# Relu work of a graph-attention layer spread over three engines instead of two

## The chip, the cores and the metric

The kernel runs on one core of a Trainium2 chip. The metric is the device time of one execution in microseconds. The core has a matrix engine (TensorE, in the profile PE for matmuls and PEld for weight loads), VectorE (DVE), ScalarE (ACT), GpSimd (POOL) and a queue that issues transfers (SP). Each engine takes its own instructions in order; semaphores hold an instruction until what it reads is there and the buffer that it writes is free.

## The reference

64 graphs (batches) of 256 nodes with 128 features pass four layers. All share one 256 x 256 matrix `adj`. Before each layer the features are normalised and clamped, and each layer's result is added to its input. All values are float32.

```python
for layer in (L0, L1, L2, L3):
    h = maximum(layernorm(x), 0)
    x = x + layer(h)

# in each layer below, x and the first h are the normalised input
# L0, five steps; both message matrices are adj, so the halves of w3, w4, w5 can be summed
m  = adj @ h
z  = sigmoid(m @ w3.T + b3 + h @ u3.T + bu3)
r  = sigmoid(m @ w4.T + b4 + h @ u3.T + bu3)
hv = tanh(m @ w5.T + b5 + (r * h) @ u5.T + bu5)
h  = (1 - z) * h + z * hv

# L1
c1 = adj.T @ x;  c2 = 2 * adj.T @ c1 - x
out = relu([x, c1, c2, c1, c2] @ Theta1 + bias)

# L2
y = (adj @ x + x) @ weight + bias;  out = y / max(norm(y), 1e-12)

# L3, e over 256 channels; W is adj: W1, W2 are its left and right 128 columns
s1 = x @ W1.T;  s2 = x @ W2.T
pre[i, j, e] = s1[i, e] + s2[j, e] + b_lin[e]
score[i, j]  = sum_e a[e] * leaky_relu(pre[i, j, e], 0.2) + adj[i, j]
out = sigmoid(softmax(score, axis=j) @ x)
```

The bulk of the work is in `score`: for every batch 256 x 256 pairs (i, j), each with 256 channels e.

## The kernel before

Two batches form a pair, 512 tokens, and 32 pairs follow one another. A token-major tile is [token % 128, batch, token // 128, feature], a feature-major one [feature, batch, token]; a [128, 512] float32 product fills one PSUM bank.

`front(p)` is a generator that computes layers 0 to 2 of a pair and, for layer 3, `s1` and `s2` (feature-major, one tile for each half k of e). In a gate step of layer 0 (lines 246 to 275) PE makes `pm`, ScalarE copies it to `mT`, PE makes `pr` and `pz` from `mT` and `hT`, ScalarE takes two sigmoids (`r`, `z`), VectorE makes `rh`, PE makes `pv`, ScalarE takes the tanh (`hv`), VectorE makes the new `hT` with a subtraction, a product and an addition (lines 265 to 268), and PE transposes it back (`pt`).

`scores(p, background)` does the bulk. leaky(v) is written as 0.2 v + 0.8 relu(v). The linear part is separable and opens the PSUM tile `pe` with six matmuls (lines 398 to 404). For the second part a slot, one r and one half k of e, handles four rows i (g = 0 to 3, 32 rows apart) of both batches: eight instructions of 256 columns write a [128, 4, 2, 256] tile `rl`, with `s1[i]` as a scalar of each partition. Every third slot is ScalarE's (line 415), the other two VectorE's (line 417). PE then reduces over e with four matmuls (line 421), one for each 32-column group of the array; a window of weights that is zero but for one column puts row i into its place. Six `rl` buffers are shared by both engines. With 32 pairs, two halves of i, 32 values of r and two halves of e there are 4096 slots. What the text calls a row is one r: two slots.

After each row `background()` advances two generators by one stage: `tail` (softmax, weighted sum and output of a finished half of i) and `front` of the next pair. So the front of pair p + 1 is interleaved with the scores of pair p; a gate step has five stages and spans five rows. The tile framework then orders the instructions of every engine with a model of its own of when operands are ready, so a background step need not stand exactly at its row.

The activation functions in use are Sqrt (norms, row norms of layer 2), Sigmoid, Tanh and Exp. Relu and copies are in line between them. Where the function set changes, a table load stands ahead of the activation. `norm_relu` (lines 166 to 182) computes statistics, Sqrt on ScalarE, a reciprocal, four scalings and a clamp on VectorE.

Of the kernel before, what the change touches and what calls it, by code (L numbers as in the profile page):

```python
# [8 lines left out]
F32 = mybir.dt.float32  # L9
AF = mybir.ActivationFunctionType  # L10
OP = mybir.AluOpType
# [4 lines left out]
NB = 2  # batches handled together: 512 tokens, one PSUM bank per [128, 512] product  # L16
# [3 lines left out]
ALPHA = 0.2  # L20


@with_exitstack
def kernel(
# [22 lines left out]
    """Four pre-norm residual graph layers over x [B, 256, 128].  # L47

    Every batch is independent, so a pair of batches goes through all four
    layers on chip. Token-major tiles are [token % 128, batch, token // 128,  # L50
    feature]; feature-major ones are [feature, batch, token].

    The last layer's scores sum a_e * leaky(s1[i, e] + s2[j, e]) over e. With
    leaky(p) = ALPHA * p + (1 - ALPHA) * relu(p) the first part is separable,
    and the second is relu on the vector and scalar engines (e on partitions,
    j along the free axis, s1[i] as the per-partition scalar), reduced over e
    by the tensor engine: a stationary [128, 32] window, zero but for one
    column that holds (1 - ALPHA) * a, puts row i into its place in PSUM.
    """
# [9 lines left out]
    relu_pool = ctx.enter_context(tc.tile_pool(name="relu", bufs=6))  # L69
    ps = ctx.enter_context(tc.tile_pool(name="ps", bufs=6, space=PSUM))  # L70
# [16 lines left out]
    ident = const.tile([P, P], F32, name="ident")  # L87
    make_identity(nc, ident)
    eps_t = const.tile([P, 1], F32, name="eps_t")
    nc.vector.memset(eps_t, LN_EPS)  # L90

    adj_n = const.tile([P, NC, N], F32, name="adj_n")  # [n, c, m]: adj[c * 128 + n, m]
    nc.sync.dma_start(adj_n, adj.rearrange("(c p) m -> p c m", p=P))
    adj_t = const.tile([P, NC, N], F32, name="adj_t")  # [m, c, n]: adj[n, c * 128 + m]
    adj_ti = const.tile([P, NC, N], F32, name="adj_ti")  # the same of adj + I
# [8 lines left out]
    def load_transposed(w, name):  # L104
        """w [128, D] or [128, 2 * D] -> its transpose, the halves summed (both multiply the same message)."""
# [11 lines left out]
        nc.vector.tensor_copy(t, pt)  # L117
# [4 lines left out]
    w4t = load_transposed(w4_w, "w4t")  # L122
    w5t = load_transposed(w5_w, "w5t")
    u5t = load_transposed(u5_w, "u5t")
# [7 lines left out]
    nc.vector.tensor_add(gate_b[:, 2:3], braw[:, 2:3], braw[:, 4:5])  # L132
    bz, br, bh = gate_b[:, 0:1], gate_b[:, 1:2], gate_b[:, 2:3]
# [25 lines left out]
    a_lin = const.tile([P, NE, N], F32, name="a_lin")  # L159
    nc.vector.memset(a_lin, ALPHA)  # L160
    for k in range(NE):
        nc.vector.tensor_scalar(win[:, k, 31:32], acol[:, k:k + 1], 1.0 - ALPHA, None, op0=OP.mult)
        nc.vector.tensor_scalar(a_lin[:, k, :], a_lin[:, k, :], acol[:, k:k + 1], None, op0=OP.mult)

# [1 line left out]
    def norm_relu(src, h):  # L166
        """h = relu(layernorm(src)) over the features, token-major."""
# [7 lines left out]
        std = work.tile([P, NB * NC], F32, name="std")  # L175
        nc.scalar.activation(std, mv[:, :, 1], AF.Sqrt, bias=eps_t, scale=1.0)
        rstd = work.tile([P, NB * NC], F32, name="rstd")
        nc.vector.reciprocal(rstd, std)
# [3 lines left out]
        nc.vector.tensor_scalar(hh, hh, 0.0, None, op0=OP.max)  # L182

    def to_feature(h, name):
        """Token-major -> feature-major, in PSUM."""
        pt = bank([P, NB, NC, P], name)
        for b in range(NB):
            for c in range(NC):
                nc.tensor.transpose(pt[:, b, c, :], h[:, b, c, :], ident)  # L189
        return pt.rearrange("p b c n -> p b (c n)")  # L190

    def to_token(ht, name):
        """Feature-major -> token-major, in PSUM."""
# [6 lines left out]
    def mix_nodes(h, a, name):  # L200
        """[f, b, n] = sum over nodes m of h[b, m, f] * a[m, n], in PSUM."""
# [6 lines left out]
    def project(pairs, name):  # L208
        """[o, b, n] = sum of w[f, o] * t[f, b, n] over the pairs (w, t), in PSUM."""
# [6 lines left out]
    def project_token(pairs, name):  # L216
        """[n, b, c, o] = sum of t[f, b, n] * w[f, o] over the pairs (t, w), in PSUM."""
# [16 lines left out]
    def front(p):  # L234
        """Layers 0 to 2 of pair p and the operands of layer 3; yields between its stages."""
        x0 = XIN.pop(p)

        # layer 0: gated message passing
# [7 lines left out]
        for step in range(STEPS):  # L246
# [4 lines left out]
            pr = project([(w4t, mT), (u3t, hT)], "pr")  # L251
            pz = project([(w3t, mT), (u3t, hT)], "pz")
            r = feat("r")
            nc.scalar.activation(r, pr, AF.Sigmoid, bias=br, scale=1.0)  # L254
            z = feat("z")
            nc.scalar.activation(z, pz, AF.Sigmoid, bias=bz, scale=1.0)  # L256
            rh = feat("rh")
            nc.vector.tensor_mul(rh, r, hT)  # L258
            yield
# [4 lines left out]
            # (1 - z) * h + z * hv = h + z * (hv - h)  # L264
            nc.vector.tensor_sub(hv, hv, hT)  # L265
            nc.vector.tensor_mul(hv, hv, z)
            hT_new = feat("hT")
            nc.vector.tensor_add(hT_new, hT, hv)
# [11 lines left out]
        # layer 1: Chebyshev hops; both hop families use adj, so their weights are summed  # L280
# [28 lines left out]
        # layer 2: (adj + I) h W + bias, rows normalised  # L309
# [14 lines left out]
        nc.vector.tensor_mul(sq, y, y)  # L324
# [160 lines left out]
```

## Time and profile before

| what | value |
|---|---|
| device time, median of 3 runs | 7429.68 us (7429.2 to 7431.93) |
| span of the profiled execution, first to last instruction | 7427.2 us |
| median less span | 2.5 us |
| busy VectorE | 6813.8 us |
| busy ScalarE | 5601.2 us |
| busy PE, as the profile models it | 7242.1 us |
| busy GpSimd | 0.7 us |
| mean granted TensorE clock | 0.995 |
| HBM read and written | 9.70 and 8.39 MB, 2 GB/s over the span |

The profiled execution's own time is its span and what lies around it; the table sets the span beside the median of the runs. In the groups of the profile a line reads: source line, engine, operation, the tile that it writes and the tiles that it reads, shapes, count, then busy microseconds in total and mean nanoseconds of one, then the idle time just before such instructions and what ended it. Instructions on one engine overlap a little, so busy time divided by the count, the distance, is less than the mean. Each float32 matmul appears as two records. The ends of matmuls are modelled, so the busy time of PE can hold waiting. Transfers are small here (2 GB/s) and are not looked at further.

### The profile page before, as it was taken

The numbers are of one execution on the slowest core, as the hardware profiler recorded it, in microseconds if no ns is written. First come the engines' busy times: TensorE is split into PE (matmuls) and PEld (weight loads), VectorE is DVE, ScalarE is ACT, GpSimd is POOL, SyncE is SP. The second block draws the span as 40 slices with busy tenths as digits, with TensorE's granted clock in tenths as the row PEclk, the third lists the DMA queues.
The fourth block names the chain that finished last, engine by engine and source line by source line (L and its number), as shares of the span: only waits on it lengthen the run. The fifth ranks groups of instructions, "written<-read, shape, count | busy, mean of one in ns | idle before, by whom it ended". The sixth has DMA issues, their size and how long they took to land.

```text
span 7427.2 us, 120750 instructions
## 1 busy us (share of the span) xinstructions
PE 7242.1 (98%) x40713; PEld 2490.1 (34%) x40713; DVE 6813.8 (92%) x25298; ACT 5601.2 (75%) x12837; POOL 0.7 (0%) x6
## 2 busy tenths in 40 slices
PE   6999999999999999999999999999999999999999
PEld 3333333333333333333333333333333333333333
DVE  4998999999999999998999999999989999999999
ACT  3777777778777777777777777777877777777777
POOL 0000000000000000000000000000000000000000
PEclk8999999999999999999999999999999999999999
DMA  0000000000000000000000000000000000000000
GB/s 13 3 4 4 3 2 3 4 4 3 2 4 3 4 3 2 4 3 4 4 3 3 3 4 4 3 2 4 3 4 3 2 4 3 4 2 2 2 2 3
DMA packets 38816, 25.83 MB, mean 3 GB/s; under 512 B 3504, under 2 KB 38192, under 8 KB 38192
## 3 DMA queue, kind: packets, MB, share of 16 engines
q1 hardware_dynamic: 35088, 17.05, 0.8%
q8 instruction: 319, 5.23, 0.3%
q14 instruction: 305, 2.50, 0.1%
q10 hardware_dynamic: 3104, 1.05, 0.1%
HBM read 9.70 MB, written 8.39 MB: 2 GB/s over the span
## 4 chain that ended last, share of the span: by engine, by line
PE 87%; DVE 12%; ACT 1%; issue 0%; DMA 0%; SPq 0%; ACTq 0%; DVEq 0%
PE pe L421 58%; PE pm L205 7%; DVE rl L417 6%; PE pr L212 4%; PE pz L212 4%; PE pv L212 4%; PE pe L403 2%; PE pe L399 2%; PE pt L197 2%; DVE h L180 1%; PE po L222 1%; PE po L381 1%; PE pa L212 1%; PE pb L212 1%; DVE stats L173 1%; PE pt L189 1%
## 5 line engine op out<-in xcount | busy, mean ns | idle before, releaser
L417 DVE TENSOR_SCALAR rl<-s,s 128x256 f32<-128x256 f32 x21848 | 5868.7, 347 | 46.8 <-PE pe L421 44.5
L421 PE MATMUL pe<-rl,win 128*32 128x512 f32 x32768 | 5102.9, 599 | 93.4 <-DVE rl L417 93.4
L415 ACT ACTIVATE rl<-s,s 128x256 f32<-128x256 f32 x10920 | 4531.2, 497 | 399.6 <-PE pe L421 394.5
L421 PEld LDWEIGHTS pe<-rl,win 128*32 128x32 f32 x32768 | 1295.7, 109 | 3162.2 <-DVE rl L417 1569.0
L205 PE MATMUL pm<-adj_t,h 128*128 128x256 f32 x1280 | 336.0, 400 | 2.8 <-ACT h L274 2.8
L258 DVE TENSOR_TENSOR rh<-r,hT 128x512 f32<-128x512 f32 x160 | 109.8, 686 | 237.9 <-ACT r L254 237.3
L205 PEld LDWEIGHTS pm<-adj_t,h 128*128 128x128 f32 x1280 | 232.4, 195 | 166.3 <-issue 78.0
L249 ACT COPY mT<-pm 128x512 f32<-128x512 f32 x160 | 93.7, 586 | 155.3 <-PE pm L205 154.3
L254 ACT ACTIVATE r<-pr,gate_b 128x512 f32<-128x512 f32 x160 | 109.9, 687 | 114.5 <-PE pr L212 114.5
L369 ACT ACTIVATE sc<-sc,nmx 128x256 f32<-128x256 f32 x128 | 64.5, 504 | 157.3 <-DVE nmx L365 156.8
L212 PE MATMUL pr<-mT,w4t 128*128 128x512 f32 x320 | 178.9, 641 | 3.5 <-ACT mT L249 3.5
L212 PE MATMUL pv<-mT,w5t 128*128 128x512 f32 x320 | 179.5, 643 | 0.0
L403 PE MATMUL pe<-a_lin,s 128*128 128x256 f32 x512 | 168.6, 419 | 0.0
L212 PE MATMUL pr<-hT,u3t 128*128 128x512 f32 x320 | 167.3, 604 | 0.0
L212 PE MATMUL pz<-mT,w3t 128*128 128x512 f32 x320 | 165.9, 600 | 0.0
L212 PE MATMUL pv<-rh,u5t 128*128 128x512 f32 x320 | 164.5, 595 | 0.0
L262 ACT ACTIVATE hv<-pv,gate_b 128x512 f32<-128x512 f32 x160 | 108.7, 680 | 73.1 <-PE pv L212 73.0
L212 PE MATMUL pz<-hT,u3t 128*128 128x512 f32 x320 | 163.4, 592 | 0.0
L256 ACT ACTIVATE z<-pz,gate_b 128x512 f32<-128x512 f32 x160 | 109.3, 683 | 64.8 <-PE pz L212 64.8
L265 DVE TENSOR_TENSOR hv<-hv,hT 128x512 f32<-128x512 f32 x160 | 109.7, 686 | 37.7 <-ACT hv L262 36.3
L403 PEld LDWEIGHTS pe<-a_lin,s 128*128 128x128 f32 x512 | 80.9, 188 | 181.4 <-issue 179.8
L399 PE MATMUL pe<-s,a_lin 128*128 128x512 f32 x256 | 141.1, 640 | 0.0
(108 smaller groups left out, 3577.9 us busy)
## 6 DMA issues: line engine op xcount, KB each, us to landing
xin<-in_x_dram SPq DMA_DIRECT2D x64, 128.0 KB, 2.2
out_dram<-o SPq DMA_DIRECT2D x64, 128.0 KB, 1.8
w_raw<-in_L_gnn_w_w_dram ACTq DMA_DIRECT2D x3, 128.0 KB, 2.6
th_raw<-in_L_gnn_Theta_dram ACTq DMA_DIRECT2D x1, 320.0 KB, 3.4
adj_n<-in_adj_dram SPq DMA_DIRECT2D x1, 256.0 KB, 4.7
w_raw<-in_L_gnn_u_w_dram ACTq DMA_DIRECT2D x2, 64.0 KB, 2.6
bias<-in_L_gnn_bias_dram ACTq DMA_DIRECT2D x2, 64.0 KB, 3.5
w<-in_L_gnn_weight_dram ACTq DMA_DIRECT2D x1, 64.0 KB, 3.1
```

Source lines behind the costliest of these rows:

```text
L197: nc.tensor.transpose(pt[:, b, c, :], ht[:, b, c * P:(c + 1) * P], ident)
L205: nc.tensor.matmul(pm[:, b, :], h[:, b, c, :], a[:, c, :], start=(c == 0), stop=(c == NC - 1))
L212: nc.tensor.matmul(pp.rearrange("p b n -> p (b n)"), w, t.rearrange("p b n -> p (b n)"), start=(k == 0), stop=(k == len(pairs) - 1))
L254: nc.scalar.activation(r, pr, AF.Sigmoid, bias=br, scale=1.0)
L256: nc.scalar.activation(z, pz, AF.Sigmoid, bias=bz, scale=1.0)
L258: nc.vector.tensor_mul(rh, r, hT)
L265: nc.vector.tensor_sub(hv, hv, hT)
L399: nc.tensor.matmul(flat, a_lin[:, k, :P], s2[k].rearrange("p b n -> p (b n)"), start=(k == 0), stop=False, skip_group_check=True)
L403: nc.tensor.matmul(pe[:, b, :], s1[k][:, b, ic * P:(ic + 1) * P], a_lin[:, k, :], start=False, stop=False, skip_group_check=True)
L415: nc.scalar.activation(rl[:, g, b, :], s2[k][:, b, :], AF.Relu, bias=sc, scale=1.0)
L417: nc.vector.tensor_scalar(rl[:, g, b, :], s2[k][:, b, :], sc, 0.0, op0=OP.add, op1=OP.max)
L421: nc.tensor.matmul(flat[g * 32:(g + 1) * 32, :], win[:, k, 31 - r:63 - r], rl[:, g].rearrange("p b n -> p (b n)"), start=False, stop=(r == ...
```

## The change

The layer-3 slots. Half k = 0 of e is done on VectorE in one instruction of 2048 columns. With s1n = -(s1 + b), relu(s1 + b + s2) = max(s2, s1n) - s1n; the last term is linear and goes into the folded terms. Its operand `s2a` stays in PSUM, in a pool of two banks of its own; `s1n` is read with a stride of zero along j. Half k = 1 goes to ScalarE as before (eight instructions) or, in 11 of 32 rows, to GpSimd, which adds and then clamps 2048 columns, both in SBUF. `rl` now has three buffers for each of the three producers.

The linear terms. One matmul with `g2` opens `pe`; the terms that depend only on i come from four one-column matmuls with `g1` and a constant `c_b` (`crow`) and are added in `tail`.

The activation table. Sigmoid becomes 0.5 tanh(v / 2) + 0.5 with the factors folded into weights, biases and the next step; Sqrt and reciprocal become a power of -0.5 on GpSimd. Exp, Tanh, Relu, Identity and copies are left.

The gates. `pz` is not computed on its own: `pr` is kept in its bank, and one matmul with w34 = w3 - w4 is added to it after `r` was read. `hv - hT` moves from VectorE to GpSimd, as do the clamp of `norm_relu`, the square and the clamp of layer 2, and the last addition of `tail`, whose result the output transfer waits for.

PSUM banks for the front go from six to four.

```diff
+POOL_ROWS = [r for r in range(32) if r * 11 % 32 < 11]
...
-    relu_pool = ctx.enter_context(tc.tile_pool(name="relu", bufs=6))
-    ps = ctx.enter_context(tc.tile_pool(name="ps", bufs=6, space=PSUM))
+    relu_pool = ctx.enter_context(tc.tile_pool(name="relu", bufs=3))
+    ps = ctx.enter_context(tc.tile_pool(name="ps", bufs=4, space=PSUM))
+    ps_s = ctx.enter_context(tc.tile_pool(name="ps_s", bufs=2, space=PSUM))
...
+    w34 = const.tile([P, P], F32, name="w34")
+    nc.vector.tensor_sub(w34, w3t, w4t)
...
+    for k in range(NE):
+        nc.tensor.matmul(pt, adj_n[:, k, P:2 * P], a_rep[:, k, :], start=(k == 0), stop=(k == NE - 1))
+    g2 = const.tile([P, P], F32, name="g2")
+    nc.vector.tensor_scalar(g2, pt, ALPHA, None, op0=OP.mult)
...
     def norm_relu(src, h):
...
-        nc.scalar.activation(std, mv[:, :, 1], AF.Sqrt, bias=eps_t, scale=1.0)
-        nc.vector.reciprocal(rstd, std)
+        nc.gpsimd.tensor_scalar(rstd, mv[:, :, 1], LN_EPS, None, op0=OP.add)
+        nc.gpsimd.tensor_tensor(rstd, rstd, minus_half, op=OP.pow)
...
-        nc.vector.tensor_scalar(hh, hh, 0.0, None, op0=OP.max)
+        nc.gpsimd.tensor_scalar(hh, hh, 0.0, None, op0=OP.max)
...
-            pr = project([(w4t, mT), (u3t, hT)], "pr")
-            pz = project([(w3t, mT), (u3t, hT)], "pz")
+            pr = project([(u3t, hT), (w4t, mT)], "pr")
             r = feat("r")
-            nc.scalar.activation(r, pr, AF.Sigmoid, bias=br, scale=1.0)
+            nc.scalar.activation(r, pr, AF.Tanh, bias=br, scale=0.5)
+            rh = feat("rh")
+            nc.vector.scalar_tensor_tensor(rh, r, 1.0, hT, op0=OP.add, op1=OP.mult)
+            yield
+            nc.tensor.matmul(pr.rearrange("p b n -> p (b n)"), w34, mT.rearrange("p b n -> p (b n)"),
+                             start=False, stop=True, skip_group_check=True)
             z = feat("z")
-            nc.scalar.activation(z, pz, AF.Sigmoid, bias=bz, scale=1.0)
+            nc.scalar.activation(z, pr, AF.Tanh, bias=bz, scale=0.5)
...
-            nc.vector.tensor_sub(hv, hv, hT)
-            nc.vector.tensor_mul(hv, hv, z)
+            nc.gpsimd.tensor_sub(hv, hv, hT)
+            nc.vector.scalar_tensor_tensor(hv, z, 1.0, hv, op0=OP.add, op1=OP.mult)
             hT_new = feat("hT")
-            nc.vector.tensor_add(hT_new, hT, hv)
+            nc.vector.scalar_tensor_tensor(hT_new, hv, 0.5, hT, op0=OP.mult, op1=OP.add)
...
-        nc.vector.tensor_mul(sq, y, y)
+        nc.gpsimd.tensor_mul(sq, y, y)
...
-        nc.scalar.activation(nrm, nrm, AF.Sqrt)
-        nc.vector.reciprocal(rn, nrm)
+        nc.gpsimd.tensor_tensor(rn, rn, minus_half, op=OP.pow)
...
+        nc.scalar.activation(s1n, pa, AF.Identity, bias=nblin[:, 0:1], scale=-1.0)
...
+        s2a = ps_s.tile([P, NB, N], F32, name="s2a")
+        nc.tensor.matmul(s2a.rearrange("p b n -> p (b n)"), adj_t[:, 1, 0:P], hT.rearrange("p b n -> p (b n)"),
+                         start=True, stop=True)
...
-            nc.vector.tensor_add(t[:, b, :], pe[:, b, :], adj_n[:, ic, :])
+            nc.vector.scalar_tensor_tensor(t[:, b, :], pe[:, b, :], crow[:, b * NC + ic:b * NC + ic + 1], adj_n[:, ic, :],
+                                           op0=OP.add, op1=OP.add)
...
-            nc.scalar.activation(o[:, b, :], po[:, b, :], AF.Sigmoid, scale=rs[:, b:b + 1])
-        nc.vector.tensor_add(o, o, x3[:, :, ic, :])
+            nc.scalar.activation(o[:, b, :], po[:, b, :], AF.Tanh, scale=rs[:, b:b + 1])
+        nc.gpsimd.tensor_scalar(o, o, 0.5, 0.5, op0=OP.mult, op1=OP.add)
+        nc.gpsimd.tensor_add(o, o, x3[:, :, ic, :])
...
+            nc.tensor.matmul(flat, g2, hT3.rearrange("p b n -> p (b n)"),
+                             start=True, stop=False, skip_group_check=True)
+            for r in range(32):
+                i0 = ic * P + r
                 for k in range(NE):
+                    e = "v" if k == 0 else "g" if r in POOL_ROWS else "s"
+                    rl = relu_pool.tile([P, 4, NB, N], F32, name="rl_" + e)
+                    if e == "s":
+                        for g in range(4):
+                            for b in range(NB):
+                                nc.scalar.activation(rl[:, g, b, :], s2b[:, b, :], AF.Relu,
+                                                     bias=s1b[:, b, i0 + g * 32:i0 + g * 32 + 1], scale=1.0)
+                    else:
+                        whole = [P, 4, NB, N]
+                        rows = (s1b if k else s1n)[:, :, i0:i0 + 97:32].rearrange("p b g -> p g b").unsqueeze(3)
+                        in0 = (s2b if k else s2a).unsqueeze(1).to_broadcast(whole)
+                        in1 = rows.to_broadcast(whole)
+                        if e == "v":
+                            nc.vector.tensor_tensor(rl, in0, in1, op=OP.max)
+                        else:
+                            nc.gpsimd.tensor_add(rl, in0, in1)
+                            nc.gpsimd.tensor_scalar(rl, rl, 0.0, None, op0=OP.max)
```

## The prediction

> **What bounds the kernel now.** I read the busy times first, then the groups of instructions, the waits, one gate step on the timeline, and three stages of one pair by windows.
>
> ```profile
> PE 7242.1 (98%) x40713; PEld 2490.1 (34%) x40713; DVE 6813.8 (92%) x25298; ACT 5601.2 (75%) x12837; POOL 0.7 (0%) x6
> L417 DVE TENSOR_SCALAR rl<-s,s 128x256 f32<-128x256 f32 x21848 | 5868.7, 347 | 46.8 <-PE pe L421 44.5
> L421 PE MATMUL pe<-rl,win 128*32 128x512 f32 x32768 | 5102.9, 599 | 93.4 <-DVE rl L417 93.4
> L415 ACT ACTIVATE rl<-s,s 128x256 f32<-128x256 f32 x10920 | 4531.2, 497 | 399.6 <-PE pe L421 394.5
> ```
>
> The 98% of PE misleads. A slot (four rows, one half of e) is 8 matmul records, so L421 took 5102.9/4096 = 1.25 us a slot on average; the timeline below has 32 records in 3.64 us, 0.91 us a slot. The waits say why:
>
> ```profile
> PEld pe L421 <- DVE rl L417: 1569.0, 3674, 2.5
> DVE rh L258 <- ACT r L254: 237.3, 51, 10.6
> ```
>
> PE's weight loads wait for VectorE's tiles; VectorE hardly waits for buffers (44.5 us). VectorE spends 8 x 268.6 ns = 2.15 us on a slot and has two of three slots.
>
> ```profile
> 3149.16 5.07 DVE L417 TENSOR_SCALAR rl<-s,s 128x256 f32<-128x256 f32 x19
> 3152.26 1.02 PE L212 MATMUL pv<-rh,u5t 128*128 128x512 f32 x2
> 3153.21 3.64 PE L421 MATMUL pe<-rl,win 128*32 128x512 f32 x32
> 3153.33 0.68 ACT L262 ACTIVATE hv<-pv,gate_b 128x512 f32<-128x512 f32 x1
> 3154.16 0.68 DVE L265 TENSOR_TENSOR hv<-hv,hT 128x512 f32<-128x512 f32 x1
> 3156.78 0.66 PE L197 MATMUL pt<-ident,hT 128*128 128x128 f32 x4
> ```
>
> A gate step repeats every 17.19 us (mT at 3144.06, then 3161.25), five rows long, with PE and VectorE both gapless. The chain hv, hT, pt has no slack.
>
> ```profile
> 3125.04:3211.00 85.96, 85.91 (x526) 30.77 (x529) 79.04 (x276) 72.65 (x163) 0.00 (x0) 1.00 0.01 3
> 3211.00:3267.90 56.90, 53.21 (x302) 19.63 (x294) 52.62 (x205) 40.12 (x92) 0.00 (x0) 1.00 0.03 8
> 3267.90:3343.20 75.30, 75.30 (x425) 23.71 (x423) 75.30 (x291) 58.59 (x140) 0.00 (x0) 1.00 0.00 1
> ```
>
> Columns: stretch, length, busy PE, PEld, DVE, ACT, POOL. These are the gates of the next pair, its layers 1 to 3, and rows with no front left. The last stretch is VectorE alone, 100%. Scores start at 138 us, the last pair alone takes 183 us; the 31 pairs between take (7427 - 138 - 183)/31 = 229.2 us each.
>
> **The change, part by part.**
>
> *VectorE.* Out go L417 (5868.7), one subtraction of each gate step (109.7), the norms' max (53.9), reciprocals (27.5), the squares and their clamp (26.9), the output add (26.8) and the s1 copies (47.9); 652 us stay. In come 2048 maxima of 2048 columns. A row pair prices them:
>
> ```profile
> L386 DVE TENSOR_TENSOR o<-o,x 128x256 f32<-128x256 f32 x64 | 26.8, 418 | 44.9 <-ACT o L385 44.9
> L265 DVE TENSOR_TENSOR hv<-hv,hT 128x512 f32<-128x512 f32 x160 | 109.7, 686 | 37.7 <-ACT hv L262 36.3
> ```
>
> 268 ns for 256 columns more, so 686 + 6 x 268 = 2.29 us; consecutive L417 overlap by 347 - 269 = 78 ns, so 2.21 us apart. PSUM as a source costs nothing visible (L363 reads it at 422 ns). VectorE: 652 + 2048 x 2.21 + 15 = 5193 us, 1620 less. But a waiting step now stands behind a 2.2 us block where it stood behind 0.27.
>
> *ScalarE.* 21 of 32 rows of the second half: 1344 slots x 3.32 = 4462 us, 69 less. All 285 table loads (365.7 us at 1.283) but the first go, as do the square roots (45); three projections' moves instead of two and the bias forms add 25. About 5146 us. These loads sat beside VectorE's work; I give them nothing but 5 us at the start.
>
> *PE.* A gate step has five projections for six: 17.19 - 0.91 = 16.28 us. Opening a half of the scores needs one matmul for six, 240 us less in all, in stretches where VectorE set the pace: nothing.
>
> *GpSimd.* It had six instructions; now 704 slots, each a sum and a clamp of 2048 columns, and the moved small steps. Two rows bound it:
>
> ```profile
> masks.py:197 POOL MEMSET ident<- 128x128 f32 x1 | 0.2, 204 | 0.3 <-POOLq L471 0.3
> masks.py:199 POOL TENSOR_SCALAR_AFFINE_SELECT ident<-ident 128x128 f32<-128x128 f32 x1 | 0.3, 292 | 0.1
> ```
>
> With some 99 ns fixed (a memset of one column), they give 0.83 and 1.52 ns a column: a clamp of 1.8 to 3.2 us, a sum, which reads twice, 3.5 to 6.3. The select does arithmetic but ran once, cold; I take the middle, 2.5 + 4.9 = 7.4 us (5.3 to 9.5). At these middle rates the moved steps cost 14 us a pair (six two-input steps of 512 columns at 1.3, four clamps at 0.7, the outputs 2.2, small ones 1.5). GpSimd: 22 x 7.4 + 14 = 177 us a pair, or 5670.
>
> The Trainium skill, GPSIMD Engine Reference, section "Elementwise — side-by-side cycle accounting", measures 4497 ns for such a sum of 2048 float32 columns and advises VectorE for elementwise work. No run here shows it; by it the sum below would be some 180 us less, about 6650.
>
> *Buffers, queues, start.* The six shared tile buffers become three for each producer, and the front has four PSUM banks for six. VectorE waited 44.5 us for buffers in the whole run, and three maxima ahead cover three rows, 7 to 8 us: nothing, as long as no wait is longer; a longer one is priced with the waits. The 64 output transfers (1.8 us each) now follow GpSimd's add instead of VectorE's; only the last is on the path, within the 10 us I keep for the end. At the start, 138 us before, the chain loses four table loads (5 us), gains five hand-overs to GpSimd (0.6 us of longer subtraction and 0.2 each, 4 us) and the small matmuls of the folded constants behind the loads (4 us): 141.
>
> *New waits.* Each gate step goes ACT hv, then GpSimd, then VectorE. Queued behind GpSimd's wait are its next slots; behind VectorE's, the next maxima, then PE. The built order has 3.6 rows on PE between pv and pt, 3.6 x 1.82 = 6.6 us. Against that: hv 0.9, subtraction 1.4, product 0.7, one max 2.2, hT 0.7, hand-overs 0.4: 6.3. It just fits. What GpSimd's reads do to VectorE's while both run, no row shows: nothing at the low end, a whole instruction of the other engine at the high end. At the high end the product waits out a sum (4.9), hT in seven of ten steps another (4.2): 23.8 us a step. I take half a sum, 2.4 us a step, 0.8 for each of its three two-input steps, because hand-overs leave GpSimd moments between instructions.
>
> The row that bears on this: L417 moves 256 columns in 347 ns, L386 takes 418. The Trainium skill, SBUF — State Buffer, section "Who interferes with whom", says that a VectorE instruction with two SBUF inputs, or in a two-port mode, and a GpSimd instruction lock each other out for a whole instruction, while one SBUF input does not contend. The max from PSUM keeps to that; the gate products do not. By the rule the high end holds: about 7790.
>
> *Sum by stage of a pair.* Gates, 25 rows: 5 x (16.28 + 2.4) = 93.4 (86.0 before). Layers 1 to 3 now lie beside 21 rows: PE 38.6 + 16.6 = 55.2; VectorE 46.4 + 9.0 = 55.4; GpSimd 7.2 slots, 53.5, plus 4.4 of moved steps, plus three norms where it waits for VectorE's scalings behind half a max (2.2 each): 64.5; five two-input steps at 0.8: 68.5. Free, 18 rows: GpSimd 11/32 x 7.4 = 2.55 a row against 2.21 (VectorE), 2.18 (ACT), 1.82 (PE): 45.9 + 2.2 = 48.1. Together 210.0 for 229.2. Whole: 141 + 31 x 210.0 + 64 x 2.55 + 10 = 6824 span, plus the 2.5 us between span (7427.2) and median (7429.7): 6826.
>
> **Rivals.**
> 1. No port wait and a slot of 5.3 us: PE bounds the gates (81.4), VectorE the rest (58 + 39.8): 179.2 a pair, 5850; with slots of 7.4, 194.0 and 6330. For it: the chain fits in 6.6 us. Against it: four engines at 160 to 177 us a pair must never miss each other.
> 2. Slower, by one mechanism: VectorE's gate products stand behind whole GpSimd sums. 119 + 74 + 48 = 241 a pair, 7790. It decides from 229 on, that is where the wait reaches 6.2 us a step (2.4 taken). For it: hT to pt had no slack before. Against: nothing in the trace shows such blocking.
> 3. GpSimd at its upper row, 9.5 us a slot: 22 x 9.5 + 14 + 7 = 231 a pair, 7520. For it: the select is the nearest kind of instruction; against: it ran once.
> 4. The max is not what it says, PSUM or not, and excludes GpSimd: 141 + 177 = 318 a pair, over 10,000.
>
> **How the numbers follow.** Forecast (6450 to 7200) 0.44; rival 1 0.25; rival 2 0.19; rival 3 0.08, half of it slower; rival 4 0.04. Within 0.2%, which is what a measurement of this kernel tells from no change: 0.02, taken from rivals 2 and 3. Faster 0.44 + 0.25 + 0.04 = 0.73, slower 0.25. The range 6100 to 7800 leaves out rival 4, the top of rival 2 and the bottom of rival 1, about 2 in 10.
>
> **What would show it.** Maxima at 2.29 us; sums and clamps of 7.4 us together; no table loads after the first; 25 gate rows in 93 us; gate products of 0.69 us. Products of 3 to 5 us mean rival 2; GpSimd busy over 95%, rival 3; maxima far over 2.3, rival 4. The prediction is wrong if the steps stretch past 23 us or GpSimd's slot past 9.

## The result and the profile after

The changed kernel takes 9438.7 us (9438.55 to 9439.15, four executions) against 7430.7 for the kernel before in the same comparison: 1.270 times as long, interval 1.269 to 1.272. The forecast was 6826 us in a range that ended at 7800. The profiled execution has a span of 9437.0 us and its own time is 9438.78. The period of a pair went from 229.2 to 293.5 us.

Busy time of each engine (microseconds, share of the span, instructions), and the chain of work that ended last, by engine and by line:

```profile
PE 6567.8 (70%) x40021; PEld 2324.1 (25%) x40021; DVE 6394.3 (68%) x4964; ACT 5153.1 (55%) x12257; POOL 7095.6 (75%) x2182
...
POOL 49%; PE 29%; DVE 14%; issue 6%; ACT 1%; DMA 0%; POOLq 0%; ACTq 0%; DVEq 0%
```

VectorE fell from 92% to 68% and ScalarE from 75% to 55%, and no engine took their place: GpSimd, with 49% of the chain the most of any engine, is busy 75%. So the engines wait for each other. VectorE's groups, with the mean duration of one instruction (ns) after the comma:

```profile
L467 DVE TENSOR_TENSOR rl_v<-s2a,s1n 128x2048 f32<-128x2048 f32 x2048 | 4607.5, 2280 | 1088.2 <-PE pe L473 1083.0 <-PE s2a L393 5.0
L307 DVE SCALAR_TENSOR_TENSOR hT<-hv,hT 128x512 f32<-128x512 f32 x160 | 370.9, 2318 | 0.5
L293 DVE SCALAR_TENSOR_TENSOR rh<-r,hT 128x512 f32<-128x512 f32 x160 | 321.9, 2012 | 103.2 <-ACT r L291 103.2
L305 DVE SCALAR_TENSOR_TENSOR hv<-z,hv 128x512 f32<-128x512 f32 x160 | 294.5, 1841 | 96.9 <-POOL hv L304 96.9
```

And GpSimd's:

```profile
L470 POOL TENSOR_SCALAR rl_g<-rl_g 128x2048 f32<-128x2048 f32 x704 | 3850.9, 5470 | 55.8
L469 POOL TENSOR_TENSOR rl_g<-s2b,s1b 128x2048 f32<-128x2048 f32 x704 | 2551.9, 3625 | 1350.1 <-PE pe L473 1342.0 <-ACT s2b L398 4.8
```

Three things stand here. The max takes what it was priced at, 2.28 us. A slot on GpSimd takes 3.62 + 5.47 = 9.1 us, and its clamp is the longer half. And the three gate steps on VectorE, 0.69 us each before, take 1.8 to 2.3 us in the mean. Two more readings follow, first the waits (total, times, longest):

```profile
ACT rl_s L459 <- PE pe L473: 1522.2, 633, 15.2
...
POOL rl_g L469 <- PE pe L473: 1342.0, 277, 8.9
DVE h L218 <- POOL rstd L216: 1155.3, 96, 22.6
...
PEld pt L227 <- POOL h L220: 1065.2, 95, 24.3
```

VectorE waits for the norms' `rstd`, 12 us at a time in the mean and up to 22.6. PE's wait for the clamped `h` is for the most part the same stretch seen from PE. Layer 2 waits 7 us for its squares (218.1 us in 32 waits); meanwhile ScalarE and GpSimd run out of buffers, which PE frees. The first norm of a pair waits longest, here as a group and once on the timeline (start, duration):

```profile
L218 DVE TENSOR_SCALAR h<-xin,mv,rstd 128x128 f32<-128x128 f32 x128 | 35.9, 343 | 681.1 <-POOL rstd L216 681.1
```

```profile
4242.11 0.17 DVE L213 BATCH_NORM_AGGREGATE mv<-stats 128x2 f32<-128x6 f32 x1
...
4242.88 5.36 POOL L470 TENSOR_SCALAR rl_g<-rl_g 128x2048 f32<-128x2048 f32 x1
...
4266.25 0.23 POOL L215 TENSOR_SCALAR rstd<-mv 128x4 f32<-128x4 f32 x1
...
4267.63 1.12 DVE L218 TENSOR_SCALAR h<-xin,mv,rstd 128x128 f32<-128x128 f32 x4 [22.62 <-POOL rstd L216]
```

The statistics are ready at 4242.28 us. GpSimd then makes a clamp and two whole slots more before it takes `rstd`. The norm's own clamp does not queue: it starts 0.09 us after the scalings (4268.84 us). Then the timeline of one gate step:

```profile
4084.90 3.62 POOL L469 TENSOR_TENSOR rl_g<-s2b,s1b 128x2048 f32<-128x2048 f32 x1 [4.07 <-PE pe L473]
4085.01 4.06 DVE L293 SCALAR_TENSOR_TENSOR rh<-r,hT 128x512 f32<-128x512 f32 x1
...
4088.61 5.68 POOL L470 TENSOR_SCALAR rl_g<-rl_g 128x2048 f32<-128x2048 f32 x1
...
4097.30 3.62 POOL L469 TENSOR_TENSOR rl_g<-s2b,s1b 128x2048 f32<-128x2048 f32 x1 [1.76 <-PE pe L473]
...
4098.38 3.08 DVE L307 SCALAR_TENSOR_TENSOR hT<-hv,hT 128x512 f32<-128x512 f32 x1
...
4101.61 0.63 PE L235 MATMUL pt<-ident,hT 128*128 128x128 f32 x4 [2.73 <-DVE hT L307]
```

`rh` starts 0.11 us after a sum on GpSimd and ends 0.55 us after that sum; `hT` starts inside the next sum and ends 0.54 us after it. Both spent the sum waiting. The max, with one operand in PSUM, is never held up so: the longest of the 2048 takes 2.29 us. The stages of one pair by windows (the columns as before; the last three are the granted clock, the DMA share and GB/s):

```profile
3982.40:4103.00 120.60, 98.95 (x529) 33.41 (x532) 85.83 (x40) 70.24 (x160) 87.11 (x25) 0.89 0.01 2
4103.00:4209.50 106.50, 66.45 (x430) 27.03 (x423) 72.73 (x80) 53.98 (x132) 78.29 (x29) 0.82 0.02 4
4209.50:4276.00 66.50, 39.63 (x302) 11.94 (x305) 41.84 (x35) 36.84 (x93) 56.41 (x15) 0.82 0.00 1
```

| stage | before | forecast | measured |
|---|---|---|---|
| gates | 86.0 | 93.4 | 120.6 |
| layers 1 to 3 | 56.9 | 68.5 | 106.5 |
| free rows | 75.3 | 48.1 | 66.5 |
| sum | 218.2 (pair 229.2) | 210.0 | 293.6 |

The windows of before lie in a pair of 223.5 us (the pairs take 223.5, 233.1 and 230.7 us in turn) and end 5.3 us short of it; those of the changed kernel cover their pair whole. Only the free rows gained. Of the 83.6 us over the forecast, 27.2 lie in the gates, 38.0 in layers 1 to 3 and 18.4 in the free rows, which end with the 22.6 us wait for `rstd` shown above.

### The profile page after: what moved, and what is told of

Its sections match the earlier page's. It is cut to its first block, busy times and chain, and to the rows that moved or that the text cites. A ratio compares the mean times of both kernels' runs of the same rounds, so it can differ in the third digit from the quotient of the medians.

```text
span 9437.0 us, 102574 instructions
## 1 busy us (share of the span) xinstructions
PE 6567.8 (70%) x40021; PEld 2324.1 (25%) x40021; DVE 6394.3 (68%) x4964; ACT 5153.1 (55%) x12257; POOL 7095.6 (75%) x2182
## 3 DMA queue, kind: packets, MB, share of 16 engines
q10 hardware_dynamic: 3104, 1.05, 0.0%
## 4 chain that ended last, share of the span: by engine, by line
POOL 49%; PE 29%; DVE 14%; issue 6%; ACT 1%; DMA 0%; POOLq 0%; ACTq 0%; DVEq 0%
POOL rl_g L470 26%; POOL rl_g L469 17%; PE pe L473 12%; PE pm L243 7%; DVE rl_v L467 5%; DVE hT L307 4%; DVE x L372 3%; PE pr L250 3%; PE pt L235 2%; POOL h L220 2%; DVE hv L305 1%; POOL hv L304 1%; PE pv L250 1%; POOL rstd L216 1%; PE pa L250 1%
## 5 line engine op out<-in xcount | busy, mean ns | idle before, releaser
L467 DVE TENSOR_TENSOR rl_v<-s2a,s1n 128x2048 f32<-128x2048 f32 x2048 | 4607.5, 2280 | 1088.2 <-PE pe L473 1083.0
L459 ACT ACTIVATE rl_s<-s2b,s1b 128x256 f32<-128x256 f32 x10752 | 4435.1, 496 | 1532.7 <-PE pe L473 1522.2
L470 POOL TENSOR_SCALAR rl_g<-rl_g 128x2048 f32<-128x2048 f32 x704 | 3850.9, 5470 | 55.8
L469 POOL TENSOR_TENSOR rl_g<-s2b,s1b 128x2048 f32<-128x2048 f32 x704 | 2551.9, 3625 | 1350.1 <-PE pe L473 1342.0
L473 PE MATMUL pe<-rl_v,win 128*32 128x512 f32 x16384 | 2861.2, 645 | 796.9 <-DVE rl_v L467 794.1
L473 PE MATMUL pe<-rl_s,win 128*32 128x512 f32 x10752 | 1976.4, 647 | 0.0
L473 PEld LDWEIGHTS pe<-rl_v,win 128*32 128x32 f32 x16384 | 544.6, 114 | 2340.0 <-DVE rl_v L467 1353.7
L473 PE MATMUL pe<-rl_g,win 128*32 128x512 f32 x5632 | 976.9, 616 | 76.6 <-POOL rl_g L470 76.6
L473 PEld LDWEIGHTS pe<-rl_s,win 128*32 128x32 f32 x10752 | 431.7, 118 | 906.2 <-issue 833.6
L218 DVE TENSOR_SCALAR h<-xin,mv,rstd 128x128 f32<-128x128 f32 x128 | 35.9, 343 | 681.1 <-POOL rstd L216 681.1
L218 DVE TENSOR_SCALAR h<-x,mv,rstd 128x128 f32<-128x128 f32 x384 | 106.7, 341 | 474.2 <-POOL rstd L216 474.2
L307 DVE SCALAR_TENSOR_TENSOR hT<-hv,hT 128x512 f32<-128x512 f32 x160 | 370.9, 2318 | 0.5
```

The costliest lines, as they stand in the source:

```text
L307: nc.vector.scalar_tensor_tensor(hT_new, hv, 0.5, hT, op0=OP.mult, op1=OP.add)
L459: nc.scalar.activation(rl[:, g, b, :], s2b[:, b, :], AF.Relu, bias=s1b[:, b, i0 + g * 32:i0 + g * 32 + 1], scale=1.0)
L467: nc.vector.tensor_tensor(rl, in0, in1, op=OP.max)
L469: nc.gpsimd.tensor_add(rl, in0, in1)
L470: nc.gpsimd.tensor_scalar(rl, rl, 0.0, None, op0=OP.max)
L473: nc.tensor.matmul(flat[g * 32:(g + 1) * 32, :], win[:, k, 31 - r:63 - r], rl[:, g].rearrange("p b n -> p (b n)"), start=False, stop=(r == ...
```

## The experiments

Three theories came from these lines. Queue: the moved small steps stand behind 9.1 us slots in GpSimd's order. Port: VectorE's steps that read SBUF stand still while GpSimd reads it. Price: 22 slots of 9.1 us are 200 us a pair, too many by themselves. A time given without an interval below is of one execution. An edit also shifts the order in which the framework places PE's work, so a difference of some tens of us is not read as an effect.

### Queue and Port, each alone and together

**e1_steps_back**: GpSimd keeps its slots, the small steps go back.

```diff
-        nc.gpsimd.tensor_scalar(rstd, mv[:, :, 1], LN_EPS, None, op0=OP.add)
-        nc.gpsimd.tensor_tensor(rstd, rstd, minus_half, op=OP.pow)
+        std = work.tile([P, NB * NC], F32, name="std")
+        nc.scalar.activation(std, mv[:, :, 1], AF.Sqrt, bias=eps_t, scale=1.0)
+        nc.vector.reciprocal(rstd, std)
...
-        nc.gpsimd.tensor_scalar(hh, hh, 0.0, None, op0=OP.max)
+        nc.vector.tensor_scalar(hh, hh, 0.0, None, op0=OP.max)
...                          # likewise hv - hT, sq, rn and the output's two steps
```

> All small steps go back from GpSimd to where they were before (subtraction, clamps, square, output addition on VectorE, the roots as Sqrt on ScalarE with a reciprocal, so table loads return); GpSimd keeps only its 704 slots. Queue theory (the small steps stood behind 9.05 us slots in GpSimd's order: VectorE waited 1155 us for the norms' roots, 218 for the squares, 161 for the row norms, PE 983 for the clamps): some 50 to 60 us a pair of 294 go, 7600 to 8000. Port theory (VectorE's steps with two SBUF inputs stand still while GpSimd reads): blocked steps stay and become more, 8900 to 9400. Price theory (22 slots of 9.05 us, 199 us a pair, are GpSimd's floor): floor 6500, the run follows whichever of the other two is left.

Measured: 8793 us, 645 less, in neither range. VectorE's groups say why:

```profile
L219 DVE TENSOR_SCALAR h<-x,mv,rstd 128x128 f32<-128x128 f32 x384 | 790.2, 2432 | 0.1
L308 DVE SCALAR_TENSOR_TENSOR hT<-hv,hT 128x512 f32<-128x512 f32 x160 | 394.9, 2468 | 0.5
...
L425 DVE TENSOR_SCALAR sums<-sums 128x2 f32<-128x2 f32 x64 | 210.4, 3288 | 26.2 <-ACT sc L422 26.2
```

The norm's scalings took 0.34 us each in the changed kernel, since GpSimd then stood waiting for their result. Now GpSimd runs slots beside them, and they take 2.4 us. The queue's wait went; the blocked time that it had kept away came.

**e5_one_pass**: the small steps stay on GpSimd; its slot becomes eight instructions that add and clamp in one pass.

```diff
+                    if e == "g":
+                        for g in range(4):
+                            for b in range(NB):
+                                nc.gpsimd.tensor_scalar(rl[:, g, b, :], s2b[:, b, :],
+                                                        s1b[:, b, i0 + g * 32:i0 + g * 32 + 1], 0.0,
+                                                        op0=OP.add, op1=OP.max)
...
-                            nc.gpsimd.tensor_add(rl, in0, in1)
-                            nc.gpsimd.tensor_scalar(rl, rl, 0.0, None, op0=OP.max)
...
```

> GpSimd makes its slots in one pass, eight instructions of 256 columns that add a scalar of each partition and clamp, in place of a sum (3.62 us) and a clamp (5.36 us) of 2048. By the moved output step (0.405 us for 256 columns of multiply and add) a slot costs 3.3 us, by the clamps (1.50 us for 512) 6.0. Price theory: 66 to 125 us a pair less of GpSimd work, shorter pieces ahead of each small step and each VectorE step, 7500 to 8300. Port theory: VectorE's steps wait for pieces of 0.4 to 0.75 us instead of 3.6: gate steps under 1.3 us. Queue theory: waits for the roots fall with the piece length, from 7 to 8 us to under 2, if the order lets a small step between pieces; if it stands behind a whole slot, they fall to 3 to 6.

Measured: 8914 us, 525 less and short of the range. The slot is no cheaper, but VectorE is free:

```profile
L459 POOL TENSOR_SCALAR rl_g<-s2b,s1b 128x256 f32<-128x256 f32 x5632 | 6417.1, 1170 | 1120.2 <-PE pe L475 1115.3
...
L293 DVE SCALAR_TENSOR_TENSOR rh<-r,hT 128x512 f32<-128x512 f32 x160 | 124.4, 777 | 107.4 <-ACT r L291 107.4
...
L218 DVE TENSOR_SCALAR h<-x,mv,rstd 128x128 f32<-128x128 f32 x384 | 106.9, 341 | 556.6 <-POOL rstd L216 556.6
```

Eight distances of 6417.1/5632 = 1.14 us make 9.1 us a slot. VectorE's total falls from 6394 to 5468 us with the same instructions: 927 us of the changed kernel were blocked time. What remains is the queue: the scalings still wait 1220 us for `rstd`.

**e4_psum_gates**: `r`, `z` and the gated product lie in PSUM, so that each gate step of VectorE reads one tile of SBUF. Nothing is moved from GpSimd.

```diff
-            r = feat("r")
-            nc.scalar.activation(r, pr, AF.Tanh, bias=br, scale=0.5)
+            pv = bank([P, NB, N], "pv")
+            nc.scalar.activation(pv, pr, AF.Tanh, bias=br, scale=0.5)
             rh = feat("rh")
-            nc.vector.scalar_tensor_tensor(rh, r, 1.0, hT, op0=OP.add, op1=OP.mult)
+            nc.vector.scalar_tensor_tensor(rh, pv, 1.0, hT, op0=OP.add, op1=OP.mult)
...                          # likewise z and the product hv
```

> Only the gates change: r, z and the gated difference lie in PSUM banks, so each of VectorE's three gate steps has one SBUF input; GpSimd's work and order are as in the changed kernel. Port theory: rh, hv and hT fall from 2.0, 1.8 and 2.3 us to 0.7, a gate step from 24.6 to about 19 us, 25 to 28 us a pair, 8600 to 8700. Queue theory: the steps fall or not, but the time does not, since the chain waits for GpSimd anyway: 9300 to 9440.

Measured: 8924 us, 514 less, between the ranges. The mechanism shows in full beside the same long sums:

```profile
L373 DVE SCALAR_TENSOR_TENSOR x<-y,rn,x 128x128 f32<-128x128 f32 x128 | 247.5, 1991 | 160.8 <-POOL rn L369 160.8
...
L293 DVE SCALAR_TENSOR_TENSOR rh<-pv,hT 128x512 f32<-128x512 f32 x160 | 109.5, 685 | 117.6 <-ACT pv L291 117.6
L308 DVE SCALAR_TENSOR_TENSOR hT<-pv,hT 128x512 f32<-128x512 f32 x160 | 108.8, 680 | 0.2
```

The steps whose second operand moved take 0.68 us again; layer 2's addition, left with two SBUF operands, still takes 1.99. It is where the operands lie, not the operation.

**e6_steps_pass**: the edits of e1 and e5 together.

> The two experiments that each took away one delay are put together: the small steps are off GpSimd, as where it keeps only its slots (8793 us), and its slot is eight one-input instructions of 256 columns, as in that run (8914 us). If the two delays simply add, 9439 - 645 - 525 = about 8270 us. If each was the other's cover (a step freed of the queue still stood behind a whole sum or clamp), what is left is the price of a slot: 22 x 9.0 to 9.4 us = 198 to 207 us a pair, so 138 + 31 x 198 to 215 + 205 = about 6500 to 7100 us, with VectorE's products, its four scalings and the factor two on the sums under 1 us each.

Measured: 6682 us, as the second reading expected; a pair takes 204.7 us.

| | small steps on GpSimd | small steps back |
|---|---|---|
| slot of two long instructions | 9439 | 8793 |
| slot of eight short ones | 8914 | 6682 |

Each edit alone is worth 525 or 645 us, both together 2756. Each delay covered the other. What is left is the price:

```profile
PE 5959.8 (89%) x40021; PEld 2156.9 (32%) x40021; DVE 5681.8 (85%) x5604; ACT 5401.6 (81%) x12606; POOL 6450.9 (97%) x5638
```

GpSimd is busy 97%, 22 x 9.16 = 202 of 204.7 us a pair. VectorE's total is 1878 us below that of e1 (7560), which differs in the form of GpSimd's slot alone: so much was blocked time there.

### Length, operation, and which of the small steps

**e10_short_pieces**: as e6, but sum and clamp stay two passes, each cut into eight.

```diff
-                            nc.gpsimd.tensor_add(rl, in0, in1)
-                            nc.gpsimd.tensor_scalar(rl, rl, 0.0, None, op0=OP.max)
+                            for g in range(4):
+                                for b in range(NB):
+                                    nc.gpsimd.tensor_add(rl[:, g, b, :], in0[:, g, b, :], in1[:, g, b, :])
...                          # then eight clamps of rl[:, g, b, :] in two such loops
```

> The small steps are off GpSimd; its slot is the sum and the clamp of the changed kernel, each cut into eight instructions of 256 columns. It separates the length of GpSimd's instruction from its form. If a blocked VectorE step waits for the end of the GpSimd instruction that is running, no wait is longer than 0.4 to 0.8 us (a 256-column piece of a sum of 3.6 us or a clamp of 5.4 us, plus its fixed part): rh, hv, hT and the scalings stay under 1.3 us in the mean, and the time is that of a price of 9.5 to 10.5 us a slot, 6700 to 7300 us. If the form does it (a sum with two inputs, a clamp in place), the steps wait for several pieces in a row, their means are 1.4 to 2.4 us as in the run with only the steps moved, and the time is 8300 to 8900 us.

Measured: 8264 us, a time that both readings miss, as the slot became dearer than either supposed:

```profile
L476 POOL TENSOR_SCALAR rl_g<-rl_g 128x256 f32<-128x256 f32 x5632 | 4769.7, 873 | 0.0
L473 POOL TENSOR_TENSOR rl_g<-s2b,s1b 128x256 f32<-128x256 f32 x5632 | 3386.9, 634 | 130.6 <-ACT s2b L400 130.6
```

The slot takes (4769.7 + 3386.9)/704 = 11.6 us and GpSimd is busy 98%: Price alone sets this time. The question of blocking is answered by VectorE's groups:

```profile
L219 DVE TENSOR_SCALAR h<-x,mv,rstd 128x128 f32<-128x128 f32 x384 | 302.4, 870 | 0.1
L294 DVE SCALAR_TENSOR_TENSOR rh<-r,hT 128x512 f32<-128x512 f32 x160 | 177.7, 1111 | 277.0 <-ACT r L292 277.0
...
L308 DVE SCALAR_TENSOR_TENSOR hT<-hv,hT 128x512 f32<-128x512 f32 x160 | 114.0, 713 | 2.2 <-PE pe L451 1.7
```

The same steps took 2.43, 1.05 and 2.47 us in e1. The longest `rh` took 1.67 us and the longest scaling 1.58, waits of 1.0 and 1.2 us, where the long instructions made them 3 to 5 for the scalings and `hT`. Some waits run over two or three pieces, and one subtraction near the start (4.08 us) over eight, so a step is not always let in at the next gap. VectorE's total, 6153 us, is 1407 below e1's: the length of GpSimd's instruction decides most of it. It is still 471 above e6's, so that the two-pass form seems to have a share as well.

**e12_affine_clamp**: the changed kernel with another operation in GpSimd's second pass.

```diff
-                            nc.gpsimd.tensor_scalar(rl, rl, 0.0, None, op0=OP.max)
+                            nc.gpsimd.tensor_scalar(rl, rl, 1.0, 0.0, op0=OP.mult, op1=OP.add)
```

> The changed kernel with GpSimd's clamp as a product with 1 and a sum with 0 in place of the maximum with 0 (the clamp of those rows is left out). Only the operation differs; bytes, inputs and outputs are those of the clamp. By the row of the output scaling (405 ns for 256 columns) it takes 2.5 to 3.0 us in place of 5.47, a slot 6.3 us in place of 9.05, and GpSimd's slots 138 us a pair in place of 199. If the price of the slot were the main cause, the time falls to 7000 to 7600 us; if queue and blocking are, they shrink with the slot only in part: 8200 to 8900 us. If the duration stays at 5.4 us, the maximum isn't what is dear.

Measured: 7690 us, 1748 less and just above the first range.

```profile
L470 POOL TENSOR_SCALAR rl_g<-rl_g 128x2048 f32<-128x2048 f32 x704 | 1416.8, 2013 | 58.3
L307 DVE SCALAR_TENSOR_TENSOR hT<-hv,hT 128x512 f32<-128x512 f32 x160 | 371.0, 2319 | 0.5
```

The same tile takes 2.01 us with a product and a sum and 5.47 with a maximum, so the maximum is what is dear. It is the largest effect of a single edit: with the shorter slot VectorE's wait for `rstd` falls from 1155 to 260 us, so the price also works through the queue. The slot is then 5.6 us, below the forecast's 7.4, and the kernel is still slower than before and 864 us above the forecast: `hT` stands behind the sum as long as ever. A price as forecast would not have saved the forecast.

**e13_norms_back**: as e6, with `hv - hT` and the output's two steps on GpSimd again.

> The run with both delays gone (6682 us), but with the gates' subtraction and the last step of the outputs on GpSimd again: of the small steps only the norms and the row norms of layer 2 are off its queue. 160 subtractions and 64 outputs then stand in GpSimd's queue behind up to one slot of 9 us. If each waits half a slot on the path, 5 x 4.5 + 2 = 25 us a pair and 7450 us; if the framework's order lets them in between slots at no loss, 6700 to 6800 us. It tells which of the moved steps the queue delay of the changed kernel came from: the norms (8914 less this) or the subtraction (this less 6682).

Measured: 7543 us, 861 above e6 and near the 7450 of half a slot of wait for each. The waits of VectorE and PE in a gate step:

```profile
PE pt L236 <- DVE hT L308: 731.0, 129, 14.9
DVE hv L306 <- POOL hv L305: 660.6, 129, 15.9
```

So of the 2232 us between 8914 and 6682, the norms and row norms are 1371 and the subtraction with the outputs 861, when they are taken off in this order.

### The change without GpSimd's slots

**e2_slots_scalar**: ScalarE takes all rows of the second half; GpSimd keeps the small steps.

```diff
-POOL_ROWS = [r for r in range(32) if r * 11 % 32 < 11]
+POOL_ROWS = []
```

> GpSimd's 11 of 32 rows go to ScalarE; everything else of the change stays, the small steps on GpSimd too. All three theories lose their cause and ScalarE becomes the bound: 64 slots x 3.32 + 21 = 234 us a pair, 141 + 31 x 234 + 212 + 10 = 7600. If instead the max from PSUM, the three-deep buffers or the fewer PSUM banks were the cause, it stays above 8500. VectorE's gate steps should be back at 0.69 us and the square clamps' waits near nothing.

Measured: 8718 us. The expectation had left out ScalarE's own hand-overs:

```profile
PE 8397.7 (96%) x40021; PEld 2543.5 (29%) x40021; DVE 5516.9 (63%) x4964; ACT 7332.8 (84%) x17889; POOL 716.4 (8%) x774
```

ScalarE's slots never wait (0.0 us idle before them); its 64 rows a pair are 208 us and all its work 229; the other 41 us of the 270 it stands at the products that the front and the tail need from PE (23 us of them in the gate steps), which come behind the rows that ScalarE itself has yet to fill. By the expectation's own mark, 8500, the max, the buffers or the banks would be to blame; the next run has the same ones and takes 7746 us, so they are not what holds this one.

**e8_no_gpsimd**: the 11 rows go to VectorE, in eight instructions as before the change (the loop of e5 on `nc.vector`). **e9_seven_rows**: the same with 7 rows.

> GpSimd keeps the small steps only; its 11 rows go to VectorE as eight instructions of 256 columns, as in the kernel before. It is the rest of the change by itself: the max from PSUM, one activation table, the folded linear terms, five projections a step. VectorE's total becomes 652 + 2048 x 2.21 + 704 x 2.15 + 160 = about 6850 us, as before the change (6814), so 7200 to 7500 us. Well over 7700 would mean that the max's 2.2 us blocks, the shallower buffers or the moved steps cost by themselves.

> As the run before it with 7 of 32 rows on VectorE and 25 on ScalarE. VectorE's total falls by 256 x 2.15 = 550 us to 6300, ScalarE's rises by 256 x 3.25 = 830 to 6000. If VectorE's total sets the time, 6800 to 7100 us; if ScalarE's hand-overs do (8718 us with all 32 rows on ScalarE), 7300 or more.

Measured: 7745.5 us (1.043, 1.041 to 1.044) and 7173.5 (0.965, 0.964 to 0.967). Neither lies in a range that was expected: e8 is over its 7500 and e9 between its two. VectorE's total in e8 is 6863.7 us, as priced, and yet it is 316 us slower than before. Two runs ask why.

**e14_vector_four**: e8 with a fourth buffer for the tiles of the max (`bufs=4 if e == "v" else 3`). **e15_vector_steps**: e8 with the small steps back, as in e1.

> The rest of the change by itself (GpSimd's 11 rows on VectorE, 7746 us, 24.7 us a pair of VectorE's period without work where the kernel before had 15.4), with a fourth buffer for the tiles of the max. If the shallower buffers cause the 316 us over the kernel before, the time falls to 7450 to 7600 us, and ScalarE's wait for PE (1278 us, 395 before) falls with it. If the hand-overs through GpSimd or the max's length do, it stays at 7700 to 7760 us.

> The rest of the change by itself, with the small steps back on VectorE and ScalarE: GpSimd has no work left. VectorE's total rises by some 300 us (6864 to about 7160), the hand-overs to GpSimd go. If the hand-overs cause the 316 us, the time falls in spite of VectorE's larger total, to 7500 to 7700 us; if they don't, VectorE's total lifts it to 7950 to 8100 us.

Measured: 7744.8 us (1.043, 1.040 to 1.046) and 7422.8 (0.999, 0.998 to 1.000).

```profile
PE 6420.8 (87%) x40021; PEld 2118.4 (29%) x40021; DVE 7047.6 (95%) x11236; ACT 5487.7 (74%) x12666; POOL 0.7 (0%) x6
```

The depth changes nothing here. The moved steps cost 323 us even on a GpSimd with nothing else to do, although they relieve VectorE of 184; without them the time is below the range that was expected. They keep GpSimd busy for 751 us in e8, so part of the 323 can be their longer duration; it was not told apart from the hand-over. With them gone, and without GpSimd, the change is worth nothing: VectorE's total is 7048 us against 6814, and it is busy 95% of the time.

### Two faster versions

**e7_eight_rows** is e6 with 8 rows on GpSimd for 11 (the first two lines below); **e11_four_buffers** adds a fourth buffer for the tiles of the max (the last line).

```diff
-POOL_ROWS = [r for r in range(32) if r * 11 % 32 < 11]
+POOL_ROWS = [r * 32 // 8 + 1 for r in range(8)]
...
+                    rl = relu_pool.tile([P, 4, NB, N], F32, name="rl_" + e, bufs=4 if e == "v" else 3)
```

> As the run before it, with GpSimd on 8 of 32 rows of the second half instead of 11 (ScalarE takes the other 24). If the price of GpSimd's slot is what then sets the time, a pair costs GpSimd 16 x 9.3 = 149 us, VectorE some 178 (64 maxima at 2.21 and 37 us of small steps), ScalarE 48 x 3.25 + 33 = 189: ScalarE's share and its hand-overs set the time, 6500 to 7000 us, and it is faster than the run with 11 rows. If buffers or PE's order of rows set it, the two take the same time.

> The run with 8 rows on GpSimd (6643 us), and a fourth buffer for VectorE's tiles. There VectorE waited 475 us for buffers, and PE's weight loads 1133 us for VectorE's tiles. If three buffers hold it back, these waits fall and the time is 6450 to 6600 us. If VectorE and PE only hand tiles over one by one (a max of 2.2 us, then 0.9 us on PE), the depth changes nothing: 6620 to 6660 us.

Measured: 6643.1 us (0.894, 0.893 to 0.895) and 6383.0 (0.859, 0.858 to 0.861). Both beat the kernel before. e7 is only 39 us below e6: GpSimd is busy 71% there and VectorE and ScalarE 85 and 90%, so the price of GpSimd's slot no longer sets the time. PE's waits for VectorE's tiles show what the buffer then does:

```profile
PEld pe L477 <- DVE rl_v L474: 1132.9, 834, 3.5
```

```profile
PEld pe L477 <- DVE rl_v L474: 584.0, 410, 2.4
```

The first is e7, the second e11: PE's wait for VectorE's tiles halves. The depth that is worth nothing in e8 is worth 260 us here, with three producers at work.

## Why the prediction was wrong

*What bounds the kernel before: right.* Taking rows from VectorE speeds the kernel up (e9), and leaving its total high leaves the time (e15).

*VectorE's max, ScalarE, tables: right.* 2.28 us for 2.29; ScalarE 5153 us for 5146; one table load is left. Without blocking VectorE's total is 6863.7 - 1569.4 (the eight-piece slots of e8) = 5294 us for the 5193 forecast. Rival 4 is out: no max was ever stretched.

*GpSimd's slot: mis-sized, and within its bounds only because two errors met.* Taken 4.9 + 2.5 us, measured 3.62 + 5.47. The sum lies at the lower row's rate, the clamp above the upper bound of 3.2. Both bounding rows, a memset and a select, hold no maximum; e12 shows that a pass of products and sums would have been 2.01. The slot alone does not make the miss: rival 3 had 9.5 us for it and came to 7520. The moved steps were put at 14 us a pair and took 715/32 = 22.

*The port wait: the right mechanism, taken too small.* The forecast took half a sum for a gate step, 2.4 us. The three rows above less 0.69 each make 4.1 us a step, 8.5 us a pair more than forecast, where the gates took 27.2 more. The rest came with the hand-over through GpSimd and was not taken apart. Rival 2's reason, whole sums, is what the timeline shows, and e4 shows that operands decide; that its 119 us for the gates lie so near the 120.6 measured is luck, as it got there with a wait of 7.5 us a step. The "moments between instructions" in which VectorE would be let in are too few with instructions of 3.6 and 5.4 us; e5 and e10 make more of them, and VectorE's steps then come back to 0.7 to 1.1 us in the mean. The Trainium skill, SBUF — State Buffer, section "Who interferes with whom", describes this lock; the runs agree with it on the two-input steps beside a sum, with 4.06 us for a step of 0.69, but some steps ended inside a clamp (last section). The GPSIMD Engine Reference, section "Elementwise — side-by-side cycle accounting", has 4497 ns for the sum; measured were 3625, with an operand of stride zero. Sums of two full tiles are nearer to it: the subtraction took 1.28 us for 512 columns and the output addition 0.73 for 256, from which an estimate for 2048 is 4.6 us. That the stride makes the difference was not tried.

*The norms' hand-over to GpSimd: the step that failed.* It was priced at 2.2 us a norm, as GpSimd's wait for VectorE, and GpSimd's own queue was given nothing. But `rstd` stands behind slots: VectorE waited 21 us for it in the first norm of a pair (681.1/32) and 5 us in each of the three others (474.2/96). With the waits for the squares and the row norms layers 1 to 3 took 106.5 us for 68.5, the largest part of the miss. The prediction named GpSimd's slots as what is queued behind the waiting subtraction, but not what the subtraction and the power are queued behind. e13 puts 1371 us on the norms and row norms and 861 on the subtraction and the outputs, once blocking is out of the way. Even with an empty queue the moved steps cost 323 us (e15 against e8).

*The free rows.* 66.5 us for 48.1, and the same step failed. By GpSimd's price a row would be 11/32 x 9.1 = 3.13 us for 2.55. But with the tiles that GpSimd had made ahead, PE takes 17 rows in the first 37 us of the stage, 2.2 us each. Then PE takes none for 23.4 us: it stands at the transposition of the next pair's first norm, whose `rstd` is behind the slots shown above. The forecast had added 2.2 us to its 18 rows.

*The chances.* Rivals 2 and 3 stood as alternatives, at 0.19 and 0.08, and ended at 7790 and 7520. Both came true at once, with a third delay that was in no rival, and they don't add: alone, each edit bought 525 or 645 us of a possible 2756. A list of single mechanisms could not reach 9439; a range that holds it would have needed two together. The 0.73 for a faster kernel fell with them. "Steps past 23 us or a slot past 9" was named as what would prove it wrong, and both happened (gate steps of 20.8 to 27 us, slots of 9.1).

## What to carry to other kernels

Before an engine gets bulk work, write down every short step in its queue that others wait for: each stands behind a whole bulk instruction, or several. Where two engines read SBUF at once, ask of each instruction how long the other's runs and where the operands lie; cut the bulk into short pieces or put an operand into PSUM. When an edit that removes a clear wait brings little, look for the second delay that it uncovers before giving the theory up: here two edits worth 525 and 645 us were worth 2756 together.

## What the runs showed of the hardware

- On GpSimd a maximum is dear: 5.36 to 5.68 us for 2048 float32 columns, 1.50 for 512, where a product and a sum in one pass took 2.01 us for 2048 (e12) and 0.40 for 256. With two operations in the pass it is dear too: an addition and a maximum took 1.17 us for 256 columns (e5). A power of 128 x 4 took 1.04.
- A tiny VectorE step can stand behind a one-input clamp too: the factor two on the sums (128 x 2 elements, 0.16 us in e2) took up to 4.6 us. A clamp that took 5.68 us for 5.36 always had a two-input step beside its start, which had waited out the sum and ended 0.5 us into the clamp (all 249 clamps over 5.5 us; 424 of the 455 others had no such step beside their start). Other steps ended inside a clamp: `hT` after 1.91 us, 1.2 us before the clamp's end; why there and not elsewhere stays open.
- The granted clock was mostly lower where PE was busy for less of the time, with the same number of matmuls: 0.849 in the changed kernel (PE busy 70%), 0.875 in e1 (74%), 0.928 in e12 (82%), 0.968 in e8 (86%), 0.993 in e6 (89%). But it was 0.987 in e10 at 85% and 0.984 in e2 at 96%, so the share alone does not set it. The matmuls of the scores took 645 ns in the changed kernel for 599 before; that the clock is the cause was not tried.
